# Softmax denominators of every second query chunk from ScalarE's accumulated exponentials

## The chip, the cores and the metric

The kernel runs on one core of a Trainium2 chip. Its engines work side by side, each through its own queue in program order: TensorE (PE in the profile; its weight loads are PEld), VectorE (DVE), ScalarE (ACT), GpSimd (POOL) and SyncE (SP), which issues most of the DMAs. The metric is the device time of one execution in microseconds; of several executions the median counts.

## The reference

It is a block of a transformer with the normalization after each part: attention without a mask, a residual and a layer norm, then a layer of eight low-rank experts of which each token uses one, a residual and a layer norm. With B = 4 sequences of S = 1024 tokens, width D = 512, 16 heads of 32, rank 64:

```
xq, xk, xv = heads(x @ wq.T), heads(x @ wk.T), heads(x @ wv.T)
probs = softmax(xq @ xk.T)                    # over the 1024 keys, no scaling
x = layernorm(x + merge(probs @ xv) @ wo.T)
logits = x @ Wr.T + br
e, weight = argmax(softmax(logits)), max(softmax(logits))
x = layernorm(x + weight * B[e] @ (A[e] @ x) / 64)
```

All of it is in 32-bit floats. The softmax takes 4 x 16 x 1024 rows of 1024 scores, and each row needs its maximum, its exponentials and their sum.

## The kernel before

**Units and steps.** A unit is a sequence b and a group g of four heads; there are 16. The queries of a unit come in four chunks of 256, the keys in eight tiles of 128. The program is a list of some 270 steps, and in step i every engine gets the work of two positions: `scores(i)`, and `weigh(i - 16)`, which works one unit behind. For the last sequence the order is turned: chunk by chunk, the four groups of a chunk after one another, so that finished chunks can go on to the experts.

**scores** (lines 280 to 297). For 128 queries and 512 keys TensorE makes the scores of four heads in four PSUM banks (L290), each from a strip of 32 rows, so that four matmuls run together. VectorE takes the maximum of each row from them (L292). After eight such steps, which are two chunks, the two halves' maxima are joined (L296), and GpSimd splits the result into three bf16 parts (`split`, L192 to L197), one column each of `spread_m`. Two steps later TensorE turns them (`turn_m`, L303) and ScalarE copies them as `mT`.

**weigh** (L313). For two key tiles and 256 queries TensorE first writes the negated maxima into four banks, as a product of ones and `mT` (L321), and adds the scores, keys down the partitions (L330). ScalarE takes the exponential of each bank (L340, 128x512), which are the weights `probs`. GpSimd adds the weights of key tile after key tile into `dens` (L343, L351), all but the last one, or for the last unit all but the last two.

**combine, settle, divide.** In every fourth step, when a chunk's eight key tiles are there, TensorE multiplies the weights with the values (L372, 32 matmuls for one bank), and ScalarE copies the result (L380). Two steps later `settle` sums over the partitions by matmuls with ones, of `dens` and of the tiles that GpSimd left out (L360), and ScalarE copies that too (L391). VectorE takes the reciprocal (L394, 128x256), and in the step after that GpSimd multiplies (L399) and has `aT`, the chunk's attention.

**PSUM.** There are eight banks, handed out in strict rotation by `bank()`. A matmul that opens a bank waits until whoever reads that bank's last content is done.

**What fills the steps.** Projections of queries, keys and values (L257, L267, L276, each followed by a ScalarE copy out of PSUM: L259, L268, L277), the product with `wo` (L455), and the experts: for the first three sequences tokens are sorted by expert through DRAM and each pair of tiles is turned (L601), taken up (L608), taken down (L617), normalized and stored (`step`, `weigh_y`, `norm_y`, `store`); the last sequence is computed for all experts at once and masked (`Last`: `project`, `norm`, `turn`, `up`, `mask`, `down`). The normalization itself is `apply` (L420) on ScalarE; its statistics are VectorE's (L415 to L417).

**What sets the order.** Each filling is a `Piece` with a cost in TensorE cycles, a first and a last step. A planner (lines 913 to 949) goes through the steps, works out a `level`, the mean cost that the steps must take for all pieces to meet their last step, and puts pieces into a step until it is reached. Steps with a combine are `busy` and get only pieces that are due. Within a step the order is `early` (loads), `ahead`, `weigh`, `scores`, `combine`, `small`, the pieces, `behind`. That order is then fixed for every engine:

```
if NS <= i < N:
    weigh(i - NS)
if i < len(maxima):
    scores(i)
if i in busy:
    u, c, _ = weights[i - NS]
    summed[u, c] = combine(u, c)
```

## Time and profile before

| | |
|---|---|
| median of 3 runs | 1534.2 us (1533.95 to 1535.69) |
| the profiled execution | 1532.2 us, its span 1530.5 us |
| granted TensorE clock, mean | 0.997 |
| GpSimd, running sums L351 and L343 | 745.3 + 150.9 us in 380 additions |
| VectorE, maxima L292 | 635.0 us in 1024 |
| ScalarE, exponentials L340 | 528.8 us in 1024 |
| TensorE, sums by ones L360 | 42.6 + 39.4 us busy |

In the profile a group is one line's instructions on one engine: output and inputs, shapes (partitions x elements), how many, their busy time together, the mean duration of one, and then the engine's idle time before them and who ended it. Instructions of one engine overlap at their edges, so the mean of one can be longer than busy time divided by their number. An fp32 matmul shows as two passes, and four of them in separate strips run together. A wait reads "who <- for whom: us in total, times, longest". The chain of work that ended last is followed back from the last instruction, at each step to what released it.

### The profile page before, as it was taken

Reading aid. Unit: us, or ns where it says so; the run is one execution under the profiler, and the core shown is the slowest. Engines: PE = TensorE matmul, PEld = TensorE weight load, DVE = VectorE, ACT = ScalarE, POOL = GpSimd, SP = SyncE. Lnnn points to the kernel's source line nnn. Section 1 sums busy time; section 2 is a strip of 40 time slices with the busy share of each in tenths; the row PEclk is TensorE's granted clock in tenths of the full one; section 3 lists DMA queues with packets and bytes.
Section 4 is the critical chain, followed back from the end, with each engine's and each line's share of the span. In section 5 each row is a group of like instructions: output and inputs, shape, how many; then the busy total and the mean of one; then the engine's idle time right before and its main releaser. Section 6 shows DMA issues by size and latency. Waiting matters only on the chain.

```text
span 1530.5 us, 37870 instructions
## 1 busy us (share of the span) xinstructions
PE 1495.6 (98%) x15571; PEld 965.1 (63%) x15571; DVE 929.0 (61%) x1733; ACT 763.2 (50%) x1583; POOL 1116.1 (73%) x939
## 2 busy tenths in 40 slices
PE   8999999999999999999999999999999999999996
PEld 6666666666666666666666666666666565665655
DVE  1556666656676457666677556766667567776323
ACT  1125555554445556555445555655445455555551
POOL 2028888877777777888777868888877777778880
PEclk9999999999999999999999999999999999999999
DMA  7431212132002423324100522441400331121000
GB/s 234 138 102 51 71 43 71 42 97 99 15 15 97 146 84 111 113 90 146 35 15 30 173 84 77 125 139 43 166 15 16 123 93 33 57 82 61 29 1 28
DMA packets 93054, 122.13 MB, mean 80 GB/s; under 512 B 7608, under 2 KB 68040, under 8 KB 92881
## 3 DMA queue, kind: packets, MB, share of 16 engines
q1 hardware_dynamic: 84672, 103.93, 21.6%
q0 software_dynamic: 6096, 13.69, 2.4%
q8 instruction: 122, 2.00, 0.6%
q10 hardware_dynamic: 2112, 2.10, 0.4%
q14 instruction: 52, 0.42, 0.1%
HBM read 92.34 MB, written 33.63 MB: 82 GB/s over the span
## 4 chain that ended last, share of the span: by engine, by line
PE 88%; POOL 4%; ACT 3%; issue 2%; DVE 2%; DMA 1%; ACTq 0%; POOLq 0%; SPq 0%; DVEq 0%
PE bank L372 14%; PE bank L290 14%; PE bank L330 13%; PE bank L276 8%; PE bank L257 8%; PE bank L267 8%; PE bank L455 7%; PE bank L321 5%; PE bank L360 4%; POOL dens L351 3%; ACT probs L340 2%; PE bank L601 2%; PE bank L617 2%; PE bank L608 2%; PE bank L729 1%
## 5 line engine op out<-in xcount | busy, mean ns | idle before, releaser
L292 DVE TENSOR_REDUCE top<-bank 128x1 f32<-128x512 f32 x1024 | 635.0, 682 | 458.9 <-PE bank L290 451.9
L351 POOL TENSOR_TENSOR dens<-dens,probs 128x1024 f32<-128x1024 f32 x316 | 745.3, 2358 | 128.7 <-ACT probs L340 116.4
L340 ACT ACTIVATE probs<-bank 128x512 f32<-128x512 f32 x1024 | 528.8, 603 | 286.2 <-PE bank L330 272.9
L290 PE MATMUL bank<-k,q 32*128 32x512 f32 x2048 | 287.1, 594 | 1.5 <-DVE whose_i L552 1.3
L330 PE MATMUL bank<-q,k 32*128 32x256 f32 x4096 | 266.9, 374 | 0.0
L372 PE MATMUL bank<-probs,v 128*32 128x256 f32 x4096 | 236.0, 381 | 0.8 <-ACT probs L340 0.8
L330 PEld LDWEIGHTS bank<-q,k 32*128 32x128 f32 x4096 | 201.4, 184 | 18.8 <-issue 3.2
L372 PEld LDWEIGHTS bank<-probs,v 128*32 128x32 f32 x4096 | 127.1, 110 | 125.9 <-ACT probs L340 47.9
L343 POOL TENSOR_TENSOR dens<-probs 128x1024 f32<-128x1024 f32 x64 | 150.9, 2358 | 62.7 <-ACT probs L340 62.4
L257 PE MATMUL bank<-xT,wq 128*128 128x256 f32 x512 | 129.2, 398 | 8.7 <-DMA xT<-in_xt 6.1
L290 PEld LDWEIGHTS bank<-k,q 32*128 32x128 f32 x2048 | 112.0, 184 | 25.8 <-issue 6.1
L267 PE MATMUL bank<-xT,wk 128*128 128x256 f32 x512 | 125.4, 389 | 1.4 <-ACT probs L340 0.9
L276 PE MATMUL bank<-wv,xT 128*128 128x256 f32 (+1 forms) x512 | 125.0, 391 | 0.6 <-ACT probs L340 0.2
L257 PEld LDWEIGHTS bank<-xT,wq 128*128 128x128 f32 x512 | 95.2, 194 | 47.4 <-ACT probs L340 25.7
L455 PE MATMUL bank<-wo,aT 128*128 128x264 f32 (+1 forms) x512 | 123.2, 389 | 1.7 <-POOL aT L399 1.7
L394 DVE RECIPROCAL both<-both 128x256 f32<-128x256 f32 x64 | 111.6, 1744 | 11.1 <-ACT both L391 11.1
L276 PEld LDWEIGHTS bank<-wv,xT 128*128 128x128 f32 x512 | 93.7, 190 | 36.6 <-ACT probs L340 18.9
L267 PEld LDWEIGHTS bank<-xT,wk 128*128 128x128 f32 x512 | 95.3, 192 | 33.8 <-ACT probs L340 21.1
L455 PEld LDWEIGHTS bank<-wo,aT 128*128 128x128 f32 x512 | 94.5, 190 | 32.8 <-ACT probs L340 16.8
L321 PE MATMUL bank<-mT,ones_b 3*128 3x512 bf16 x1024 | 107.5, 384 | 3.1 <-ACT probs L340 1.5
L380 ACT COPY both<-bank 128x256 f32<-128x256 f32 x64 | 23.9, 373 | 157.6 <-PE bank L372 151.6
L635 POOL DMA_INDIRECT out<-x x48 | 49.5, 1032 | 53.8 <-DMA out<-x 35.3
(124 smaller groups left out, 1038.4 us busy)
## 6 DMA issues: line engine op xcount, KB each, us to landing
xT<-in_xt SPq DMA_DIRECT2D x98, 512.0 KB, 3.6
sorted<-nothing SPq DMA_DIRECT2D x12, 1028.0 KB, 7.4
x<-sorted SPq DMA_DIRECT2D x48, 257.0 KB, 3.0
h<-in_x SPq DMA_DIRECT2D x32, 256.0 KB, 4.6
wa<-in_wa SPq DMA_DIRECT2D x48, 128.0 KB, 2.6
wb<-in_wb SPq DMA_DIRECT2D x48, 128.0 KB, 3.6
out<-h SPq DMA_DIRECT2D x8, 256.0 KB, 2.0
wo<-in_wo POOLq DMA_DIRECT2D x1, 1024.0 KB
```

The lines of the kernel that those rows point to most:

```text
L257: pe.matmul(ps, wq_sb[:, c, ts(units[u][1], P)], x.x[:, c, :], start=(c == 0), stop=(c == C - 1))
L267: pe.matmul(ps, wk_sb[:, c, ts(units[u][1], P)], x.x[:, c, :], start=(c == 0), stop=(c == C - 1))
L276: pe.matmul(ps, x.x[:, c, ts(t, P)], wv_sb[:, c, columns(h)], start=(c == 0), stop=(c == C - 1))
L290: pe.matmul(ps, q[r, ts(t % TQ, P)], kT[u][r, ts(n, 512)], start=True, stop=True)
L292: dve.tensor_reduce(top[i][:, here // 2, j, n : n + 1], ps, axis=AX.X, op=ALU.max, negate=True)
L321: pe.matmul(ps.rearrange("p (k q) -> p k q", q=QC), ones_b[r, :], m[r, :].unsqueeze(1).to_broadcast((NP, 2, QC)), start=True, stop=False,)
L330: pe.matmul(ps[:, ts(k, QC)], kT[u][r, ts(2 * kp + k, P)], qT[u, c][r, :], start=False, stop=(k == 1),)
L340: act.activation(pr[:, :, j, :], ps.rearrange("p (k q) -> p k q", q=QC), AF.Exp)
L343: pool.tensor_add(dens[u, c], pr[:, 0].rearrange("p j q -> p (j q)"), pr[:, 1].rearrange("p j q -> p (j q)"),)
L351: pool.tensor_add(dens[u, c], dens[u, c], pr[:, k].rearrange("p j q -> p (j q)"))
L372: pe.matmul(ps[j * HD : (j + 1) * HD, :QC], v[:, k, col : col + HD], probs[u, c, k // 2][:, k % 2, j, :], start=(k == 0), stop=(k == NK - 1),)
L455: pe.matmul(ps, aT[b, c, n][:, ts(i, P)], wo_sb[:, c, columns(half)], start=(c == 0), stop=(c == C - 1))
```

## The change

The chunks are taken in pairs, which share one `spread_m`. For the second chunk of each pair the sum of the weights is computed while its maxima are: ScalarE takes the exponential of the scores once more, from the banks of `scores`, with the maximum of that half row as its bias, and sums along the row (`accum_out`); the exponentials themselves go to a tile `junk` that nobody reads. When both halves are known, the sums are scaled to the common maximum and added, and VectorE takes the reciprocal (`invert`, one step later). The reciprocal goes the way of the maximum: it is split into three bf16 parts, in three more columns of `spread_m`, and turned by the same matmuls. For that chunk `combine` spreads it over the partitions by four bf16 matmuls with a constant `pick`, copies it, and VectorE multiplies it with the combined values. For the first chunk of a pair GpSimd now adds all eight key tiles, and `settle` (four matmuls, a reciprocal in PSUM, a multiply, all on VectorE after that) runs four steps after its combine, in the step in which the other chunk is combined.

The maxima of the two chunks take turns, step by step, so that the steps with exponentials of scores are the odd ones. Copies of q, k and v go from ScalarE to VectorE. `apply` goes to GpSimd, but for the last chunk of all. The planner's level is 1500 cycles higher in one of four steps (an odd one without a combine) and 750 lower in the others, queries may be projected a unit earlier, and the first and last steps and the gaps of the fillings behind a chunk become shorter. The core of the diff:

```diff
+    maxima = [(maxima[s - s % TS + s % 2 * KP + s % TS // 2], s % 2 * KP + s % TS // 2) for s in range(len(maxima))]
+    def summed_early(s):
+        return s % TS >= KP
...
-        act.copy(qT[u, x.n], ps)
+        dve.tensor_copy(qT[u, x.n], ps)
...
         for j, ps in enumerate(tiles):
-            dve.tensor_reduce(top[i][:, here // 2, j, n : n + 1], ps, axis=AX.X, op=ALU.max, negate=True)
+            dve.tensor_reduce(top[i][:, at, j, n : n + 1], ps, axis=AX.X, op=ALU.max, negate=True)
+        if at >= TQ:
+            for j, ps in enumerate(tiles):
+                act.activation(
+                    junk[:, j % 2, :],
+                    ps,
+                    AF.Exp,
+                    bias=top[i][:, at, j, n : n + 1],
+                    accum_out=sums[i][:, at - TQ, j, n : n + 1],
+                )
         if here == TS - 1:
+            m = spread_from[i % 2]
+            less = work.tile([P, TQ, GH, 2], F32, tag="less", name="less")
+            dve.tensor_reduce(m[:, :, :, 0], top[i], axis=AX.X, op=ALU.min)
+            dve.tensor_sub(less, m[:, TQ:, :, 0:1].to_broadcast((P, TQ, GH, 2)), top[i][:, TQ:])
+            act.activation(less, less, AF.Exp)
+            room[i] = m, less
+
+    def invert(i):
+        m, less = room[i]
+        dve.tensor_mul(less, less, sums[i])
+        dve.tensor_reduce(m[:, TQ:, :, 1], less, axis=AX.X, op=ALU.add)
+        dve.reciprocal(m[:, TQ:, :, 1], m[:, TQ:, :, 1])
+        split(m, [spread_m[i % 2][:, :, :, p : 2 * NP : NP] for p in range(NP)], "mrest")
...
+    def settle(s):
+        u, c, _ = weights[s]
+        b, g = units[u]
+        ps = bank()[:, :QC]
+        for j in range(GH):
+            pe.matmul(ps[j * HD : (j + 1) * HD, :], ones, dens[u, c][:, ts(j, QC)], start=True, stop=True)
+        dve.reciprocal(ps, ps)
+        aT[b, g, c] = work.tile([P, QC], F32, tag="aT", name="aT", bufs=15)
+        dve.tensor_mul(aT[b, g, c], ps, both[u, c])
+
+    def combine(s):
...
+        if summed_early(s):
+            ps = bank()[:, :QC]
+            for j in range(GH):
+                pe.matmul(
+                    ps[j * HD : (j + 1) * HD, :],
+                    pick[:, j, :],
+                    mT[s // TS][:, ts(s % TS // KP, QC)],
+                    start=True,
+                    stop=True,
+                )
+            inv = work.tile([P, QC], F32, tag="inv", name="inv", bufs=1)
+            dve.tensor_copy(inv, ps)
...
+        if summed_early(s):
+            aT[b, g, c] = work.tile([P, QC], F32, tag="aT", name="aT", bufs=15)
+            dve.tensor_mul(aT[b, g, c], ps, inv)
+        else:
+            both[u, c] = work.tile([P, QC], F32, tag="both", name="both", bufs=1)
+            act.copy(both[u, c], ps)
...
+    def apply(h, rs, i, eng=pool):
+        scale, shift = rs[:, 0, i : i + 1], rs[:, 1, i : i + 1]
+        if eng is act:
+            act.activation(h, h, AF.Identity, bias=shift, scale=scale)
+        else:
+            eng.tensor_scalar(h, h, scale, shift, ALU.mult, ALU.add)
...
     for i in range(len(weights) // TS):
+        later(TS * i + TS, 0, invert, i, where=ahead)
         later(TS * i + TS + 2, 512, turn_m, i)
...
+        level += 1500 if i % KP == 1 else -750
...
         if i in busy:
-            u, c, _ = weights[i - NS]
-            summed[u, c] = combine(u, c)
+            if summed_early(i - NS):
+                settle(i - NS - KP)
+            combine(i - NS)
```

## The prediction

> **What bounds the kernel now.** I read the busy times first, then the groups, the waits, the chain in a middle stretch, and the order of time in one step.
>
> ```profile
> span 1530.5 us, 37870 instructions
> PE 1495.6 (98%) x15571; PEld 965.1 (63%) x15571; DVE 929.0 (61%) x1733; ACT 763.2 (50%) x1583; POOL 1116.1 (73%) x939
> ```
>
> TensorE is busy for 98% of the span, at a granted clock of 0.997. Busy is not proof, so the waits decide:
>
> ```profile
> DVE top L292 <- PE bank L290: 451.9, 202, 24.2
> ACT probs L340 <- PE bank L330: 272.9, 226, 4.5
> ```
>
> In 202 of 256 steps VectorE stood waiting for the scores, and before 226 exponentials ScalarE stood waiting for TensorE. So TensorE sets the pace, and what it is spared is gained, until another engine makes it wait. The chain that ended last, in a middle stretch (start, us, what):
>
> ```profile
> 599.69 0.33 PE bank L321 x4
> 600.01 0.86 PE bank L330 x16
> 600.88 0.86 PE bank L290 x8
> 601.74 1.03 PE bank L360 x16
> 602.76 1.93 PE bank L257 x8
> ...
> 612.95 3.59 PE bank L372 x64
> ```
>
> A step is 0.33 + 0.86 + 0.86 = 2.05 us, then its fillings: 1.93 for a projection (1.75 for a second one), 3.59 for a combine in every fourth step, 1.03 for a settle. The same step in order of time elsewhere:
>
> ```profile
> 1100.69 0.40 PE L321 MATMUL bank<-mT,ones_b 3*128 3x512 bf16 x4
> 1100.92 1.03 PE L330 MATMUL bank<-q,k 32*128 32x256 f32 x16
> 1101.78 1.03 PE L290 MATMUL bank<-k,q 32*128 32x512 f32 x8
> 1102.06 2.07 ACT L340 ACTIVATE probs<-bank 128x512 f32<-128x512 f32 x4 [2.64 <-PE bank L330]
> 1102.85 2.47 DVE L292 TENSOR_REDUCE top<-bank 128x1 f32<-128x512 f32 x4
> ```
>
> Counted from the step's start: exponentials from 1.37 to 3.44 (0.52 each), maxima from 2.16 to 4.63 (0.62 each). A score bank is free today at 4.63 at the latest. The rows that price the change:
>
> ```profile
> L360 PE MATMUL bank<-probs,ones 128*32 128x256 f32 x544 | 42.6, 390 | 0.0
> L360 PE MATMUL bank<-dens,ones 128*32 128x256 f32 x512 | 39.4, 380 | 2.0 <-POOL dens L351 1.9
> L394 DVE RECIPROCAL both<-both 128x256 f32<-128x256 f32 x64 | 111.6, 1744 | 11.1 <-ACT both L391 11.1
> L420 ACT ACTIVATE x<-x,rs 128x512 f32<-128x512 f32 x48 | 36.8, 827 | 2.3 <-POOL rs L410 2.2
> 1497.95 1.52 ACT L420 ACTIVATE h<-h,rs 128x512 f32<-128x512 f32 x2 [11.51 <-POOL rs L410]
> ```
>
> **What TensorE is spared.** L360 has 544 + 512 = 1056 passes, 66 lots of 16 at 1.03: 68 us. Afterwards 32 settles of 8 passes stay, 0.52 each, and 32 picks of four bf16 matmuls of 256 columns come. The pick lies between 0.16 (half of L321's 0.33 for four of 512 columns) and 0.40 (L303, four of 128 columns that do not overlap: 0.40 in the order of time); I take 0.25. 32 x 0.77 = 25, so 43 us go (38 to 46). Both new items stand right ahead of the combine, in its tile shape. At the end the last division (copy, settle, reciprocal 1.75, multiply 0.72) made TensorE idle for 1.7 us; now one multiply of some 0.4 remains, under matmuls that need it last: 2 us. Spared: 45.
>
> **Waits that go.** In the stretch from 1442 to 1466 the chain is 69% GpSimd's L351: the running sums, 2.36 each, came too late for steps that hold little else. The four steps from 1446 to 1466 took 20 us, and their matmuls at the prices above 12. GpSimd's additions fall from 380 to 224, by 156 x 2.358 = 368 us, so I take 7 of the 8. At 1369 and 1377 the normalizations (L420, 0.76 each) stood ahead of exponentials on ScalarE; 84 of 88 go to GpSimd: 3 us. Together 10 (0 to 13).
>
> **What ScalarE gets.** 512 exponentials of scores, with a per-partition bias and a summed output, four in every odd step. Each waits for VectorE's maximum; queued behind it are the next step's exponentials and the copies of u, xsT and both, and TensorE waits for the banks of all of these. No row has this form. Below: 0.52, as L340. Above: 0.95, the 0.76 of L420, with two per-partition operands, and 0.19 for delivering the sum, as ScalarE's smallest activation (L436, 188 ns). I take 0.73: one such operand is half of the way from 0.52 to 0.76, and half of the 0.19. In total that is 374 us, against 174 us taken away (copies of q, k, v 72, of the sums 25.5, half of L380 12, L420 64): busy 763 becomes some 970, not a bound as a whole. In an odd step it is: 2.07 + 2.92 = 4.99, done 6.36 after the step's start.
>
> With eight banks in rotation the next step's scores need the last of these banks 1.19 us into that step, so an odd step shorter than about 5.2 makes TensorE wait. Most odd steps are long enough: two projections 5.7, combine 5.6 or 6.4. In the changed order 19 are not. Six have one projection (3.96): 1.03 each. Three hold an expert's up and its transposes (4.25) and seven also the down matmuls (5.3), with 1.36 of copies more on ScalarE: 2.1 and 1.05 each. Three others lack 5.2 together. Sum 25 us (9 at 0.52; at 0.95, 42 and more, see the rival).
>
> The Trainium skill, "ScalarE: Activation LUTs" (section "What ACT_TABLE_LOAD costs"), speaks against the move: a per-partition operand adds about 93 ns to an ACTIVATE. L340 to L420, with two of them, agrees roughly, 0.24 us a pair. By the page alone, with 0.61 and no price for the sum, the 25 would be an estimated 16 and the forecast 1511.
>
> **What VectorE gets.** 192 copies at about 0.40 (L457, PSUM to SBUF, 0.42 or 0.38 in a row), 77 us; 32 reciprocals fewer, minus 56; 96 short multiplies and copies, 38; 128 tiny ones at 0.2, 26. Busy 929 becomes some 1015. The copies stand behind the step's maxima and hide in the idle time that L292 shows. But all of the division falls into the 32 steps that settle two chunks: maxima until 4.63, minimum and difference 0.4, reciprocal 1.74, then three of some 0.42, the last at 8.1. The next step's scores want that bank at 6.4 + 1.2 = 7.6: 0.45 each, 14 us (0, if the eight banks happen to stand better, to 30). The expert steps hold 5.98 of VectorE's work against 5.3: 2 us for what spills over.
>
> GpSimd loses also 47 us of divisions (L399) and gains 84 normalizations, each between 0.6 (an 8x512 cast on GpSimd, 602 ns) and 1.2 (half of L351): 50 to 100 us. They stand ahead of its scatters and stores, at most a few us later; that, the five splits now after the reciprocal, and the loads that SP issues in another order (DMA share at most 0.39 from 90 us on) hide behind steps of slack: nothing, at worst 5 us.
>
> The skill's "TensorEngine Tiling (Array Packing)", section "PSUM Bottleneck", warns that packing speeds TensorE but not the emptying of PSUM. This case has both engines on score banks twice in odd steps. Applied to every odd step rather than to 19, with 0.45 us lost in each of 128, it would make an estimated 58 in place of the 25 and the time 1553.
>
> **Sum.** -45 - 10 + 25 + 14 + 2 = -14. The profiled execution took 1532.2 (span 1530.5 and 1.7 around it) and becomes 1518; the median of the runs is 2.0 above it, 1534.2, so I forecast 1520.
>
> **Rivals.**
> 1. ScalarE becomes the bound of odd steps: an exponential with its sum costs 0.95. Then the 19 steps lose 42; in the 32 combines without a settle ScalarE's copy frees its bank at 7.7 against 6.8, 0.88 each, 28 us; the 33 steps of two projections lose 0.45, 15; with 14 and 2 that is 101 against 55, so 1580. The balance tips at about 0.80, where the 19 steps and the copies cost 39. For it: L420 at 0.76 without any sum. Against it: L420 has two operands and writes what it reads.
> 2. ScalarE behind VectorE: the reciprocal of settle steps (VectorE 6.4 of 6.5 us) delays the next maxima, and every expert step does, so that exponentials wait. If each of 32 settles costs 1.0 instead of 0.45 and 12 expert steps 0.7, that is 24 us more: 1544. For it: at 1278 to 1288 the chain already runs through VectorE. Against it: VectorE waits for TensorE before 202 maxima.
> 3. The settles were no loss, or all of the gain returns as waits for banks: 1534. Against it: the chain passes through L360 in order, 1.03 us at a time.
> 4. Everything hides: 0.52 each, and no wait after the reciprocal: -55 + 9 + 2, so 1490.
>
> **How the numbers follow.** A difference of 0.2% is about what a measurement of this kernel can tell. The forecast's own case (1503 to 1530) has 0.46; rival 4 has 0.12; rival 3 has 0.08; rival 2 has 0.19; rival 1 0.15, some of it between its tipping point and its full price. Faster 0.58, same 0.08, slower 0.34. Most of 1 lies above 1558 and half of 4 below 1497: the range is 1497 to 1558.
>
> **What would show it.** The ones-times-sums matmuls fall to 256 passes. The new exponentials' row shows four in about 2.9 us; over 3.25 says rival 1, and TensorE's waits then name ScalarE. TensorE busy falls to some 1460 to 1480. VectorE's own idle before the maxima should stay above 300 us; if not, and if ScalarE waits mainly for VectorE, it is rival 2. In the last 90 us GpSimd should leave the chain. I would be wrong first in the 0.73 or in the 0.45.

## The result, and the profile after

The changed kernel takes 1540.85 us (median of six runs, 1538.29 to 1544.62), the kernel before 1534.25 in six runs beside it: a ratio of 1.0043 (95% interval 1.0027 to 1.0059). It is slower by 0.4%, where 1520 was forecast. Two later comparisons gave 1.0058 (1.0045 to 1.0071) and 1.0046 (1.0030 to 1.0063). The profiled execution took 1541.39 us at a granted clock of 0.989. One run of those below, the fourth of a_noscatter_2, took 2412.57 us at a granted clock of 0.556 and is left out.

The page of the changed kernel, its span and its busy times:

```profile
span 1539.4 us, 37695 instructions
PE 1493.6 (97%) x14899; PEld 972.3 (63%) x14899; DVE 1008.9 (66%) x2117; ACT 946.4 (61%) x2267; POOL 772.3 (50%) x809
```

VectorE's 1009 and ScalarE's 946 lie near the foretold 1015 and 970. TensorE's 1494 does not lie near its 1460 to 1480: it runs 672 instructions fewer (of the sums' 1056 passes 256 are left, as foretold) and is as busy as before. Matmuls that wait for a bank show as busy time here: the same 2048 passes of scores have 316.2 us (L319) where they had 287.1 (L290). So part of the gain has gone into such waits. The lower mean clock goes with the stalls: from 104.7 to 480 us it is 1.00 as before, and from 497 to 507 us, where engines stand still, 0.73; in a_noscatter_2, a run below without that stall, it is 1.00 there too. Its view of waits, the lines that carry the comparison (us in total, times, longest):

```profile
DVE top L321 <- PE bank L319: 303.4, 201, 6.3
...
DVE top L321 <- remote: 12.6, 1, 12.6
...
PE bank L370 <- ACT junk L324: 5.0, 17, 0.5
...
PE bank L739 <- POOL h L468: 3.3, 1, 3.3
PE bank L405 <- POOL dens L397: 3.2, 1, 3.2
```

VectorE still waits for TensorE before 201 maxima, as foretold. New are TensorE's 17 waits for the score exponentials. Its waits for GpSimd should have left and grew, to 3.3 and 3.2 us from 1.9 and 1.7. VectorE has one wait of 12.6 us, where it had one of 6.6, until "remote", a releaser that the profile can't name. The new exponentials, four in the order of time:

```profile
283.27 0.71 ACT L324 ACTIVATE junk<-bank,top 128x512 bf16<-128x512 f32 x1
283.84 0.23 ACT L324 ACTIVATION_READ_ACCUMULATOR junk<-bank,top 128x1 f32 x1
283.93 0.72 ACT L324 ACTIVATE junk<-bank,top 128x512 bf16<-128x512 f32 x1
284.50 0.24 ACT L324 ACTIVATION_READ_ACCUMULATOR junk<-bank,top 128x1 f32 x1
284.60 0.73 ACT L324 ACTIVATE junk<-bank,top 128x512 bf16<-128x512 f32 x1
```

One exponential and its sum are two instructions that overlap; the next pair starts 0.66 us later (283.27, 283.93, 284.60). I had priced it at 0.73.

To find where the time went I split the span into steps, each from its first L370 matmul (L321 in the kernel before) to that of the next step, and took from each step its matmuls at the prices of the prediction: 2.05 for the step, 1.93 for a projection and 1.75 for a second one, 3.59 for a combine, 1.02 for an expert's transposes or up, 1.05 for its down matmuls, 0.4 for the turned maxima. What is left is waiting, plus the settling, which is left in so that it can be compared. Sorted by kind of step, in us (number of steps), from the profiled executions:

| kind of step | before | changed |
|---|---|---|
| settling (with its matmuls) | 53.4 (49) | 21.7 (23) |
| the step after a settling | 4.9 (47) | 14.2 (24) |
| the step after a short odd step (under 5.2 us of matmuls) | -0.1 (1) | 24.0 (18) |
| around the scatters (steps 88-95, 150-159, 214-223) | 18.7 (28) | 29.7 (28) |
| steps from 240 on | 9.0 (31) | 6.9 (31) |
| combines without a settling, and others | 11.8 (99) | 12.1 (131) |

The first exponentials' step starts at 104.69 instead of 99.84: 1.5 of it is the first load of xT (TensorE's wait for it 7.6 against 6.1), the rest two projections (3.65 together) that the planner now does earlier and that are missing later. After the last step 48.0 us follow, against 51.6.

### The profile page after: what moved, and what is told of

It is laid out like the page before. It is cut to its first block, busy times and chain, and to the rows that moved or that the text cites. A ratio compares the mean times of both kernels' runs of the same rounds, so it can differ in the third digit from the quotient of the medians.

```text
span 1539.4 us, 37695 instructions
## 1 busy us (share of the span) xinstructions
PE 1493.6 (97%) x14899; PEld 972.3 (63%) x14899; DVE 1008.9 (66%) x2117; ACT 946.4 (61%) x2267; POOL 772.3 (50%) x809
## 4 chain that ended last, share of the span: by engine, by line
PE 85%; ACT 5%; issue 4%; DVE 2%; POOL 2%; DMA 1%; SPq 0%; ACTq 0%; POOLq 0%; DVEq 0%
PE bank L431 15%; PE bank L319 14%; PE bank L379 14%; PE bank L283 8%; PE bank L302 8%; PE bank L293 8%; PE bank L503 6%; PE bank L370 5%; ACT probs L389 4%; PE bank L762 2%; PE bank L777 1%; ACT junk L324 1%; PE bank L665 1%; PE bank L656 1%; POOL dens L397 1%
## 5 line engine op out<-in xcount | busy, mean ns | idle before, releaser
L321 DVE TENSOR_REDUCE top<-bank 128x1 f32<-128x512 f32 x1024 | 636.1, 683 | 318.3 <-PE bank L319 303.4
L389 ACT ACTIVATE probs<-bank 128x512 f32<-128x512 f32 x1024 | 529.2, 605 | 414.0 <-PE bank L379 405.9
L397 POOL TENSOR_TENSOR dens<-dens,probs 128x1024 f32<-128x1024 f32 x192 | 452.8, 2358 | 86.0 <-ACT probs L389 77.1
L324 ACT ACTIVATE junk<-bank,top 128x512 bf16<-128x512 f32 x512 | 347.8, 717 | 76.1 <-DVE top L321 75.9
L319 PE MATMUL bank<-k,q 32*128 32x512 f32 x2048 | 316.2, 600 | 2.5 <-DVE whose_i L600 1.2
L379 PE MATMUL bank<-q,k 32*128 32x256 f32 x4096 | 274.4, 378 | 1.1 <-issue 1.1
L431 PE MATMUL bank<-probs,v 128*32 128x256 f32 x4096 | 237.9, 384 | 4.7 <-ACT probs L389 3.9
L211 POOL CAST sm<-sf 128x32 bf16<-128x32 f32 x32 | 8.2, 256 | 423.5 <-DVE sf L345 404.0
L379 PEld LDWEIGHTS bank<-q,k 32*128 32x128 f32 x4096 | 204.8, 186 | 22.8 <-issue 7.5
L431 PEld LDWEIGHTS bank<-probs,v 128*32 128x32 f32 x4096 | 128.3, 111 | 114.3 <-ACT probs L389 32.3
L319 PEld LDWEIGHTS bank<-k,q 32*128 32x128 f32 x2048 | 129.3, 186 | 37.2 <-DVE aT L440 6.9
L370 PE MATMUL bank<-mT,ones_b 3*128 3x512 bf16 x1024 | 115.7, 386 | 6.1 <-ACT junk L324 5.0
L324 ACT ACTIVATION_READ_ACCUMULATOR junk<-bank,top 128x1 f32 x512 | 121.5, 237 | 0.0
L370 PEld LDWEIGHTS <-ones_b 3*128 3x128 bf16 x1024 | 28.6, 91 | 97.8 <-issue 97.2
```

The lines of the kernel that those rows point to most:

```text
L319: pe.matmul(ps, q[r, ts(t % TQ, P)], kT[u][r, ts(n, 512)], start=True, stop=True)
L321: dve.tensor_reduce(top[i][:, at, j, n : n + 1], ps, axis=AX.X, op=ALU.max, negate=True)
L324: act.activation(junk[:, j % 2, :], ps, AF.Exp, bias=top[i][:, at, j, n : n + 1], accum_out=sums[i][:, at - TQ, j, n : n + 1],)
L370: pe.matmul(ps.rearrange("p (k q) -> p k q", q=QC), ones_b[r, :], m[r, :].unsqueeze(1).to_broadcast((NP, 2, QC)), start=True, stop=False,)
L379: pe.matmul(ps[:, ts(k, QC)], kT[u][r, ts(2 * kp + k, P)], qT[u, c][r, :], start=False, stop=(k == 1),)
L389: act.activation(pr[:, :, j, :], ps.rearrange("p (k q) -> p k q", q=QC), AF.Exp)
```

## The experiments

Kernels of one group ran together on one chip; each is given as a ratio to the kernel before in the same group. In the group of a_level, a_noscatter, a_norm_dve and a_pace the kernel before took 1525.16, in the others 1531.4 to 1533.4.

### What ScalarE's part costs

```
-            sums[i] = work.tile([P, TQ, GH, 2], F32, tag="sums", name="sums")
+            sums[i] = all_one
...
-        if at >= TQ:
-            for j, ps in enumerate(tiles):
-                act.activation(
...
```

> The changed kernel without its 512 exponentials of scores (L324); their sums are replaced by a constant 1, so the denominators of every second chunk are wrong, and the time holds everything of the change but this work of ScalarE. Theory A (ScalarE's turn in the odd steps is the largest cost, through score banks that come free late, through the choice's exponential that queues behind it, and in the stretch from 487 to 507 us): the 19 short odd steps give back about 1.1 to 1.4 us each, 22 to 25, the three steps 78, 82 and 86 some 5, the stretch 487 to 507 up to 8. The time falls from 1541 to 1503 to 1513. Theory B (the loss lies with VectorE, GpSimd and the loads, and ScalarE's part is the foretold 25 or less): 1518 to 1530, and the stretch 487 to 507 us keeps its 20 us.

Measured: 1519.41 us, ratio 0.9911 (0.9881 to 0.9941), so 20 us below the changed kernel by ratios. That lies in theory B's range, and so does its place: the step after a short odd step falls from 24.0 us to 7.1, the settling and what follows it keep their times (22.8 and 13.9), and steps 91 to 93 still take 25.2 us against 26.4. Step by step the difference is what the prediction had priced. The six odd steps with one projection cost the next step 0.86 to 1.13 each (foretold 1.03); three with up and transposes 2.22, 2.13 and 1.69 (2.1); six of the seven with down as well 0.9 to 1.09 (1.05). The chain of the changed kernel (start, us, what) behind one of the first kind:

```profile
294.17 0.86 PE bank L379 x16
295.04 1.90 PE bank L319 x7
```

And the chain of a_nosum there:

```profile
292.83 0.86 PE bank L371 x16
293.69 0.86 PE bank L320 x8
```

The scores (L319, here L320) take 1.90 instead of 0.86, because their last banks are still held by ScalarE. One place had not been priced: in the steps 78, 82 and 86 VectorE stands inside the choice of experts for ScalarE's small exponential, which is queued behind the four large ones, 1.0 us each time.

### What a settling costs

```
-            [probs[u, c, k // 2][:, k % 2] for k in range(added(u), NK)]
-            + [dens[u, c].rearrange("p (j q) -> p j q", q=QC)],
+            [dens[u, c].rearrange("p (j q) -> p j q", q=QC)],
```

> The kernel before with TensorE summing only the running sum (16 passes, 1.03 us) in each chunk and leaving out the one or two key tiles that GpSimd had not added; the sums lack those tiles, everything else is as it was. It measures by itself what a pass spared on TensorE is worth. 544 of 1056 passes go: 34 lots at 1.03 are 35 us. Theory A (TensorE sets the pace): 1534 becomes 1498 to 1502. Theory B (the time comes back as waits for banks, sums or copies): 1515 to 1530.

Measured: 1518.02 us, ratio 0.9911 (0.9886 to 0.9935): 13.6 us, where theory A says 34 and theory B 4 to 19, so theory B. The prediction halves a settling of 16 passes, 1.03, to 0.52. The chain of this kernel:

```profile
594.93 0.05 issue
594.98 0.64 PE bank L360 x8
```

Eight passes take 0.64, with 0.05 ahead of them. So a settling gets 0.3 shorter and not 0.5, some 19 us in all of them by the profile, and 5 of these do not reach the end. The same in the changed kernel (settling L405, pick L417, then the combine), with the scores of the step behind it:

```profile
1098.00 0.57 PE bank L405 x8
1098.57 0.11 PE bank L417 x4
1098.68 0.18 issue
1098.86 3.66 PE bank L431 x64
1102.52 0.33 PE bank L370 x4
1102.84 0.86 PE bank L379 x16
1103.71 1.43 PE bank L319 x8
```

A step that settles has a median of 6.57 us, one that only combines 5.64: 0.93 where I had 0.77. The combine (L431) is 0.18 late and 0.07 longer than before. The 1.43 in the last line is the price of the divisions on VectorE, 0.57 over the usual 0.86: the last two weight loads of these scores wait until its last multiply (L440), which is queued behind the reciprocal.

```
+            if summed_early(i):
+                later(i + NS + 1, 4 * QC, settle, i - KP)
...
-            if summed_early(i - NS):
-                settle(i - NS - KP)
             combine(i - NS)
```

> The changed kernel with the settling of the even chunk one step later, so that its reciprocal (1.76 us on VectorE) no longer stands in the step of two divisions. Theory A (the 0.45 us foretold for each of 32 steps are really lost; the step after a settling took about 0.7 longer than its matmuls): 14 to 20 us faster than the changed kernel, 1521 to 1527. Theory B (VectorE's reciprocal only moves to the next step's maxima, or was hidden): within 4 us of 1541. The order of the pieces shifts a little with it (the short odd steps go from 26 to 23, up to 4 us), so less than 5 us of gain decides nothing.

Measured: 1580.04 us, ratio 1.0312 (1.0290 to 1.0334): 40 us slower than the changed kernel, outside both theories. The chain shows why:

```profile
624.29 0.91 PE bank L319 x8
625.19 0.61 DVE top L321
625.81 0.57 issue
626.38 1.28 DVE top L321 x2
627.66 1.68 DVE bank L406
629.34 0.02 issue
629.36 0.43 DVE aT L408
```

The reciprocal works in the settling's bank, and that bank is free only after four maxima, 1.68 and 0.43 on VectorE. One step later nothing long stands between: TensorE is through with its step and waits from 625.2 to 629.8. In the changed kernel the combine's 3.59 us cover this. The step after a settling lost 38.1 us in 24 steps instead of 14.2. The 0.45 of the prediction is thus the remainder of a good place, and not a loss that a later place would spare.

### GpSimd at the end

```
-    def apply(h, rs, i, eng=pool):
+    def apply(h, rs, i, eng=act):
```

> The changed kernel with all 88 normalizations on ScalarE, as before the change (827 ns each there against 772 on GpSimd). Theory A (GpSimd's queue, with the normalizations in front of the running sums and of the transposes' input, makes TensorE wait 3.3 at 1378 and 3.2 at 1463, with a lower clock behind each): the two waits go, 5 to 10 us faster, 1531 to 1536. Theory B (ScalarE is the fuller engine in these steps, so the normalizations delay its exponentials): 2 to 8 us slower, 1543 to 1549.

Measured: 1550.83 us, ratio 1.0120 (1.0099 to 1.0140), some 10 us slower than the changed kernel: theory B, and more. The step of the settling at 1463 does fall from 11.30 to 7.74, but four steps earlier a combine takes 10.00 instead of 4.78.

```
-                apply(self.h[i], self.rs, i, pool if self.n < NQ - 1 else act)
+                apply(self.h[i], self.rs, i, dve if self.n < NQ - 1 else act)
```

> The changed kernel with the normalizations of the last sequence (12 of 16 are on GpSimd) on VectorE. Theory A (at 1319 to 1328, 1378 and 1463 TensorE waits behind GpSimd's queue, in which these normalizations, 772 ns each and up to 1.5 together, stand with the experts' and with the running sums): the waits for h and for dens go, 6 to 10 us faster, 1531 to 1535. Theory B (the running sums themselves are what is late, or VectorE is as full as GpSimd in these steps): within 3 us of 1541.

Measured: 1535.09 us, ratio 1.0067 (1.0050 to 1.0084): by ratios no better than the changed kernel on other chips. The unaltered kernel did not run on that chip, so by the total nothing is decided, but its profile can be compared step by step: step 263 falls from 11.30 to 6.52 us, and step 260 grows from 3.12 to 12.25. VectorE in that step, in order of time:

```profile
1441.37 5.02 DVE L468 TENSOR_SCALAR h<-h,rs 128x512 f32<-128x512 f32 x2 [8.39 <-POOL rs L454]
```

It waits at the head of its queue for a statistic (L454) that GpSimd gets to only behind its sums. Whichever engine normalizes, the sums decide. The chain of the kernel before in the same stretch:

```profile
1451.18 2.35 POOL dens L351
1453.54 0.68 POOL aT L399
1454.22 2.33 POOL dens L351
1456.55 0.04 issue
1456.60 0.64 PE bank L360 x8
```

And that of the changed kernel:

```profile
1454.98 2.35 POOL dens L397
1457.33 1.52 POOL h L468 x2
1458.85 2.33 POOL dens L397
1461.18 0.07 issue
1461.24 2.35 POOL dens L397
1463.60 0.04 issue
1463.64 0.72 PE bank L405 x8
```

```
+            eng = dve if s >= len(weights) - NS else pool
...
-                    pool.tensor_add(dens[u, c], dens[u, c], w)
+                    eng.tensor_add(dens[u, c], dens[u, c], w)
```

> The changed kernel with the running sums of the last 16 steps (16 additions of 2.36 us on GpSimd) on VectorE, which has no maxima any more there. Theory A (halving GpSimd's additions over the whole kernel did not help at the end: an even chunk now needs all 8 tiles, 18.9 us, while its four steps hold some 16 us, and the settling at 1463 waits for them): steps 256 to 263 fall from 34.7 us to 28 to 30, 4 to 7 us faster than the changed kernel. Theory B (the wait at 1463 is for the normalization and the transposes' input, and VectorE only takes the additions' place in the queue): less than 2 us.

Measured: 1535.35 us, ratio 1.0010 (1.0002 to 1.0019), so 6.4 us less than the unaltered kernel beside it (1541.79): theory A. Steps 256 to 263 took 30.0 us instead of 34.8 (33.1 in the unaltered kernel beside it), and TensorE no longer waits for the sums. The profile has 14 of these additions and not 16: seven for a chunk of eight tiles, 16.5 us and not 18.9. Some 3 us of the difference of the two profiles lie elsewhere, in step 220 (8.4 for 11.5), where the edit changes nothing.

```
+        eng = dve if s >= len(weights) - NS else pool
...
-            pool.tensor_add(
+            eng.tensor_add(
...
-                    pool.tensor_add(dens[u, c], dens[u, c], pr[:, k].rearrange("p j q -> p (j q)"))
+                    eng.tensor_add(dens[u, c], dens[u, c], pr[:, k].rearrange("p j q -> p (j q)"))
```

> The kernel before with the running sums of its last 16 steps on VectorE, and nothing of the change. Theory A (the sums of 2.36 us each on GpSimd made TensorE wait between 1442 and 1466, as the chain of waits says): 5 to 9 us faster than the kernel before, and the chain leaves GpSimd there. Theory B (TensorE waits there for something else next): less than 2 us.

Measured: 1536.00 us, ratio 1.0015 (1.0006 to 1.0025): theory B. Steps 259 to 265 do take 28.8 us instead of 33.5, so GpSimd's sums cost the kernel before some 5 us there. But step 258 grows from 5.33 to 11.14: the sums, now on VectorE, delay its masking, and TensorE waits for that. So the run shows what the wait held, 5 us, but not that all of it would stay if the sums had gone from both engines. The line in its view of waits:

```profile
PE bank L730 <- DVE lu L725: 4.1, 2, 3.5
```

### The scatters

VectorE in the changed kernel's profile, two lines that follow each other in order of time:

```profile
490.50 2.48 DVE L321 TENSOR_REDUCE top<-bank 128x1 f32<-128x512 f32 x4
505.60 2.71 DVE L321 TENSOR_REDUCE top<-bank 128x1 f32<-128x512 f32 x4 [12.62 <-remote]
```

GpSimd in the same stretch:

```profile
485.65 9.64 POOL L397 TENSOR_TENSOR dens<-dens,probs 128x1024 f32<-128x1024 f32 x4 [1.29 <-ACT probs L389]
495.47 1.14 POOL L604 DMA_INDIRECT sorted<-h,slot_i  x1 [0.18 <-issue]
496.91 1.00 POOL L604 DMA_INDIRECT sorted<-h,slot_i  x1 [0.30 <-issue]
...
504.61 0.98 POOL L604 DMA_INDIRECT sorted<-h,slot_i  x1 [0.30 <-issue]
```

Eight scatters follow one another from 495.47 to 505.59, and VectorE starts its next maxima at 505.60, though their scores began at 498.0 and were done before 501. So of its 12.62 us some 7 are a stall; ahead of them it had no scores. In the kernel before the first four scatters of the third sequence ran from 1203.5 to 1208.5, with a wait of 6.62 until "remote" on VectorE.

> The changed kernel once more, unaltered, on the chip of the three runs beside it. In the profiled execution of the changed kernel VectorE stood for 12.6 us until 'remote' at 493 to 506, in that of the kernel before for 6.6 at 1203 to 1209; in four later executions of kernels with the same scatters, on another chip, there was no such wait. Theory A (that stall belongs to the change: eight scatters with nothing between them): the wait of 9 us or more is there again, and the ratio to the kernel before is 1.004 as in the first comparison. Theory B (it comes and goes with the execution and hits both kernels): the wait is absent or elsewhere, steps 91 to 93 take 16 to 18 us, and the ratio stays within 1.002 to 1.006 even so, since the kernel before is spared its own.

Measured, with nothing edited: 1541.79 us, ratio 1.0058; VectorE's wait is there again (11.95 us, until 504.93, before the train ends at 505.59). Theory A.

```
-            i = pool.indirect_dma_start(
-                out=sorted_x[self.b],
...
-                in_=self.h.pop(t),
...
-            self.scatters.append(i)
+            self.h.pop(t)
```

> The changed kernel without the 24 scatters of tokens (L604): the experts of the first three sequences read empty rows and their stores go nowhere, so the output of these sequences is missing; every other instruction is there. Theory A (a train of scatters on GpSimd with nothing between them is what holds VectorE for 12.6 us and ScalarE for 3.3 at 493 to 506, and something like it at 155 and 220): steps 91 to 93 fall from 26.4 us to 15 to 17, steps 155 to 157 and 219 to 221 lose 2 to 7 each; 14 to 20 us faster, 1521 to 1527, and the waits named 'remote' go. Theory B (the stall is VectorE's chain of the count, L575 to L600, and the copies behind it): steps 91 to 93 keep at least 22 us, and the time stays above 1535.

Measured: 1522.40 us, ratio 0.9980 (0.9971 to 0.9990). But on this chip the kernel before was 6 to 8 us faster than elsewhere, and none of the four profiles of this group has a wait until "remote", with scatters or without: in a_level and a_norm_dve, which have the same train of eight, steps 91 to 93 take 18.0 us. So this run doesn't tell the theories apart.

```
-                        then += [(5 + k // 4, 0, r.scatter, k) for k in range(NT)]
+                        then += [(5 + k // 4 if b else 10 + k // 2, 0, r.scatter, k) for k in range(NT)]
...
-                end + (20 + 4 * k if b < B - 2 else 19 + 3 * k),
-                after=[(p, 3 if k else 9)],
+                end + (20 + 4 * k if b == 1 else 23 + 3 * k if b == 0 else 19 + 3 * k),
+                after=[(p, 3 if k else 9 if b else 15)],
```

> The changed kernel with the first sequence's scatters five and more steps later, two in each of the steps 96 to 99, where GpSimd adds running sums between them; the experts of that sequence begin 5 steps later. Theory A (it is the train of eight scatters with nothing between that holds VectorE and ScalarE; the kernel before has its scatters in the same steps as running sums, in trains of four, and loses 2 to 7 us): steps 91 to 93 fall from 26.4 us to about 16, and steps 96 to 99 lose at most 3; 6 to 10 us faster, 1531 to 1535. Theory B (each scatter costs its time wherever it stands): steps 96 to 99 lose what 91 to 93 gain, within 3 us of 1541.

Measured: 1540.56 us, ratio 1.0093 (1.0075 to 1.0112), on the same chip. In this form the first expert's loads went out before the last two scatters, so some of its rows are not the sequence's own. For lack of the stall on that chip it says nothing on its cause; the later experts cost some time of their own. The open question was taken up again with four kernels on one chip:

> The changed kernel unaltered, beside the next three on one chip. Where VectorE's wait until 'remote' at 493 to 506 is there, the time is 1.004 to 1.006 of the kernel before; where it is absent, theory A (the wait is part of the loss) says 1.000 to 1.002, theory B (it is not) still 1.004 to 1.006.

Measured: 1540.02 us, ratio 1.0046. The wait is there, in other places: 6.7 us on ScalarE and 5.4 on VectorE, in step 93, which takes 12.18 us.

> The changed kernel without its 24 scatters, once more, on the chip of the unaltered one beside it (the first three sequences' experts read empty rows and their stores go nowhere, so the output lacks them). Theory A (the scatters make the waits until 'remote' and the losses at 91 to 93, 154 to 157 and 219 to 221): no such wait, 12 to 17 us faster than the unaltered kernel. Theory B (only the count's chain on VectorE is at fault): less than 4 us.

Measured: 1520.39 us (three runs), ratio 0.9928 (0.9907 to 0.9949): by ratios 18 us below the unaltered kernel beside it, and no wait until "remote". Theory A.

> The kernel before without its 24 scatters, with the same part of the output missing. Theory A (in the kernel before GpSimd's running sums stand between its scatters, and they cost it less): 4 to 8 us faster than the kernel before (its one long wait until 'remote' was 6.6). Then the scatters are worth 6 to 11 us of the difference between the two kernels. Theory B (they cost both the same): 12 us or more.

The same edit in the kernel before. Measured: 1524.51 us, ratio 0.9946 (0.9930 to 0.9963): 8 to 9 us, a little above theory A's. By ratios the scatters cost the changed kernel some 10 us more than the kernel before, give or take 5; the whole difference between the two kernels is 7 here. Without scatters the changed kernel is the faster one by some 3 us, which lies within the intervals. In the profiles 7 of the 10 us lie in the steps around the scatters, 5 of them in the first sequence, where the train of eight is.

The edit of a_pace with 16 in place of 15 steps, so that all scatters stand ahead of the loads:

> The changed kernel with the first sequence's scatters two in each of the steps 96 to 99, between GpSimd's running sums, and that sequence's experts 7 steps later (in the earlier form the first expert's loads went out before the last two scatters). Theory A (a train of eight with nothing between is what costs): where the unaltered kernel beside it waits until 'remote' at 493 to 506, here steps 91 to 93 take 16 to 18 us and 96 to 99 lose at most 3, so 6 to 10 us faster than it. Theory B (the scatters cost the same anywhere): within 3 us of it.

Measured: 1536.89 us, ratio 1.0024 (1.0012 to 1.0035), 3.1 us below the unaltered kernel: at theory B's edge by the total, and theory A's by the place. Steps 91 to 93 take 18.0 us (24.7 in the unaltered kernel beside it), steps 96 to 99 lose 1 us, and no wait until "remote" is left on VectorE. The second sequence's stretch lost 4 us more, where its experts now stand in other steps. GpSimd in this kernel, sums and scatters in turn:

```profile
521.39 1.14 POOL L604 DMA_INDIRECT sorted<-h,slot_i  x1 [0.18 <-issue]
522.83 1.00 POOL L604 DMA_INDIRECT sorted<-h,slot_i  x1 [0.30 <-issue]
523.83 4.82 POOL L397 TENSOR_TENSOR dens<-dens,probs 128x1024 f32<-128x1024 f32 x2
528.80 1.00 POOL L604 DMA_INDIRECT sorted<-h,slot_i  x1 [0.15 <-issue]
```

So scatters that go out two at a time between sums cost next to nothing (0.9 us), and eight in one train cost 6.7 us, on the chips that show the stall at all. Steps 91 to 93 take 24.7 us in a_again_2, against 18.0 here and without scatters (a_noscatter_2). The 26.4 of the first profile hold 1.7 more, from another cause: step 91 took 9.92 us there, at a granted clock of 0.83, and so it did in a_noscatter without a scatter (9.97). What holds VectorE and ScalarE during a train isn't shown by any run; in a_choose_behind VectorE stands idle for 10.2 us beside the train, and the profile names TensorE's projection as the releaser. Even without scatters step 91 takes 8.29 us against 6.34 in the kernel before: that is the count's chain on VectorE (L575 to L600), now ahead of a step with less in it.

### Versions

```
-        level += 1500 if i % KP == 1 else -750
+        level += 2200 if i % KP == 1 else -1100
```

> The changed kernel with the planner's odd steps filled further (+2200 and -1100 in place of +1500 and -750), nothing else. Of the 18 short odd steps (under 5.2 us of matmuls) between the first exponentials and the last stage 3 are left (69, 133, 197). Theory A (a short odd step makes the next step wait for ScalarE, 1.0 us behind one projection or an expert's up, down and transposes, 2.1 behind up and transposes): about 14 of them go, so 14 to 18 us, 1523 to 1528. Theory B (the time lost there comes back at the next narrow place: even steps become emptier, and VectorE or the score banks then wait there): 0 to 6 us, 1535 to 1541.

Measured: 1526.20 us, ratio 1.0001 (0.9992 to 1.0011). By ratios that is 6 to 9 us less than the changed kernel on other chips, at theory B's edge or beyond; but the unaltered kernel did not run on this chip, where the stall at the scatters is absent, so the ratio is a poor measure. With the steps around the scatters left aside the waits of the two profiles differ by some 9 us. The steps behind short odd ones lose 5.3 us instead of 24.0, so theory A holds for the place; of the 19 us some are lost again, most plainly at step 262, which takes 12.06 us because TensorE waits 8.9 for GpSimd's normalization.

```
-                later(i + abs(gap), cost, f, *args, where=ahead if gap < 0 else small)
+                where = behind if f.__name__ == "choose" else ahead if gap < 0 else small
+                later(i + abs(gap), cost, f, *args, where=where)
```

> The changed kernel with the choice of experts (L481 to L488) issued behind the projections of its step instead of ahead of them, for the first three sequences. Theory A (VectorE waits inside the choice for ScalarE's small exponential, which is queued behind the four score exponentials, and the projection's sum L505 stands behind that: 1.0 us in each of the steps 78, 82 and 86 and their like in each sequence): 3 to 9 us faster over the three sequences. Theory B (the wait only moves to the next step's maxima): within 2 us.

Measured: 1542.33 us, ratio 1.0049 (1.0032 to 1.0065): theory B. Steps 78, 82 and 86 each get 0.5 to 0.6 shorter and the steps ahead of them 0.4, and around the scatters 4 us are lost again.

> The changed kernel with four things together: odd steps filled further as in the run on the levels (there 6 us), the last running sums on VectorE, the choice behind the projections, and the experts' normalizations and stores one step later, as they stood before the change. If the losses add up as priced (6, 4 to 7, 3 to 9, and 0 to 4 of the 3.2 us that the transposes' input waited at 1378): 13 to 22 us faster than the changed kernel, a ratio of 0.990 to 0.996 to the kernel before. If they hide one another, no better than 1.000.

The edits of a_level, a_adds_dve and a_choose_behind, and

```
-                then=[(-1, 0, r.weigh_y, k - 2), (1, 0, r.norm_y, k - 2), (2, 0, r.store, k - 2)] if k >= 2 else [],
+                then=[(-1, 0, r.weigh_y, k - 2), (2, 0, r.norm_y, k - 2), (3, 0, r.store, k - 2)] if k >= 2 else [],
```

Measured: 1527.10 us, ratio 0.9961 (0.9947 to 0.9976), 14.7 us below the unaltered kernel beside it, at the lower end of the 13 to 22.

> The changed kernel with three things together, one for each cause found: odd steps filled further (6 us), the last running sums on VectorE (6), and the first sequence's scatters between GpSimd's running sums (3). If they add up: 15 us faster than the changed kernel, about 1526, a ratio of 0.994 to 0.996 to the kernel before. If they hide one another: 0.998 and more.

The edits of a_level, a_adds_dve and a_pace_2. Measured: 1525.80 us, ratio 0.9947 (0.9933 to 0.9961): faster than both kernels, by 0.5% than the one before. They add up in the total. Its profile (of the longest of its five runs, 1531.02) still has a wait until "remote", now in the second sequence (step 157, 15.06 us), whose scatters are not spread.

## Why the prediction was wrong

The sign was wrong, by 21 us. Against the terms of the sum:

| term | foretold | measured | from |
|---|---|---|---|
| settling and pick on TensorE | -43 | -37 | 66 lots at 1.01, less 32 at 0.93 |
| the tail | -2 | -3.6 | 48.0 for 51.6 |
| the start | 0 | +1 | 4.85 later, less 3.65 of matmuls moved there |
| waits that go | -10 | 0 to +3 | GpSimd's waits at 1378 and 1463; steps from 240 on |
| ScalarE | +25 | +20 | a_nosum |
| VectorE in the settling | +14 | +16 | 0.59 less 0.10, in 32 steps |
| GpSimd, loads, spill | +2, at worst 5 more | +10 | b_noscatter against a_noscatter_2 |
| sum | -14 | +6 to +9 | the medians: +6.6 |

The right-hand column adds terms from profiles and from ratios of runs, each good to some us; that the sum fits so well is partly luck.

**What held.** The two numbers that I named as most doubtful were good. The exponential with its sum comes every 0.66 us, where 0.73 was taken out of 0.52 to 0.95; the row of the profile that the prediction asked for (four in some 2.9 us) shows 2.65. So rival 1 falls. The places of the loss (odd steps under 5.2 us) and their prices, 1.03, 2.1 and 1.05, were met nearly one by one; only the "three others (5.2 together)" did not lose. That is partly luck. By the prediction's own terms the first price is 6.36 - 1.19 - 3.96 = 1.21 and not 1.03, and with 0.66 in place of 0.73 it is 0.93: two errors nearly cancel. The page "ScalarE: Activation LUTs" of the Trainium skill (section "What ACT_TABLE_LOAD costs") gives 93 ns for the operand. The trace is near it: L324 took 717 ns and L389 605, so 0.11 us, though L324 also writes bf16 and sums. By that figure alone an exponential would come every 0.61 us, an estimate; the rows show 0.66, with the separate read of the sum (237 ns) in it. The warning of "TensorEngine Tiling (Array Packing)" (section "PSUM Bottleneck") would have made an estimated 58 of the 25, and a_nosum measured 20. a_settle_later shows a loss of that kind: TensorE waited while VectorE kept a bank for 2.1 us.

**What failed first: "the waits that go, -10".** The step reads "GpSimd's additions fall from 380 to 224, by 156 x 2.358 = 368 us, so I take 7 of the 8". That is an average over chunks of two kinds. The odd chunks lost all of their additions and the even ones gained one, seven for six: a chunk that GpSimd sums now needs all eight tiles, since TensorE no longer takes the last, so its additions come one after the other at 2.36 us as they did before. Where the steps are short, from 1449 to 1463, the chain runs through L397 just as it had run through L351. a_adds_dve shows that it is these sums. Less their settlings (8 of 1.03 before, 3 of 0.93 now) the steps from 240 on lost some 3 us more than before, where 10 less was foretold. The 8 was also misread: from 1446 to 1466 the kernel before does the matmuls of five steps and not of four, 17 us and not 12 at the prediction's prices, so that 3 us were to be had there; b_adds_dve found 4.7 in the steps 259 to 265. And in that run VectorE's masking was late next. The prediction named the wait and did not ask what stood behind it.

**Second: "nothing, at worst 5" for what is moved on GpSimd and SP.** I had the scatters a few us late and hidden by steps of slack. In the kernel before running sums lay between them in most places. In the first sequence of the changed kernel they fall into a chunk that has no sums, so GpSimd issues all eight in one train, and VectorE and ScalarE stand beside it. By a_noscatter_2 and b_noscatter all scatters together cost some 10 us more than before, 5 of them in this place. The DMA share, which I put at 0.39 at most, was 0.50 from 840 to 880 us in the kernel before; whether the loads cost anything no run shows. It was to be seen in the changed order of GpSimd's instructions that the sums between the scatters were gone; what a train costs was to be guessed at best from the one wait of 6.62 in the profile of before.

**Third: "32 settles of 8 passes stay, 0.52 each", the pick 0.25.** The eight passes took 0.57 (0.64 in b_fewer_sums, against 1.00 for 16) and the pick only 0.11, together less than the 0.77. What the term left out is behind them: the combine waits 0.18 for the last exponential and takes 0.07 longer. 0.93 instead of 0.77 in 32 steps is 5 us.

**Of the rivals** 2 and 3 came nearest by the time (1544 and 1534) and neither is the cause: VectorE's loss was the foretold one, and the banks' too. (The 24 us of rival 2 are 26 by its own terms, 32 x 0.55 + 12 x 0.7.) What did not come was gains, 16 us of them, and a loss of 10 at the scatters had no term.

## What to carry to other kernels

When work is halved on an engine, ask in which order the remaining half comes: where it was dense, it may stay as dense as it was, and an average saving does not reach that place. Look also at what the removed instructions had been keeping apart, for a queue without them may send a train of transfers. And before a wait is counted as gain, name the engine that is late next; one run that takes away that wait in the kernel before, as b_adds_dve does, would have shown that 5 us lay there and that VectorE was next.

## What was not expected of the hardware

- Beside a train of eight scatters (1.0 us of GpSimd each, 1.3 apart) VectorE stood idle for 11.2 to 12.6 us in three executions, some 5 of them for want of scores. In the changed kernel's profile it started again with the train's end (505.60 and 505.59), in other executions between 3.0 us before it and 1.7 behind it. On one chip two kernels with the same train (a_level, a_norm_dve) lost nothing there, and the kernel before was 6 to 8 us faster, about what it gains elsewhere when its scatters are left out (8 to 9).
- The same short stop of TensorE (1.2 us in step 91, behind the count's chain on VectorE) was followed by a granted clock of 1.00 in some executions (step 91: 8.28 us, a_again_2, a_level) and by 0.83 in others (9.9 us, a_again, a_noscatter).
- Halving the passes of a short group of matmuls (16 to 8, 128x32 by 128x256) took its time in the chain from 1.00 to 0.64.
- On VectorE a normalization of 128x512 took 546 ns in the median of 12, but four that ran beside GpSimd's sums took 1.7 to 2.6 us. Each of these four ended 0.28 us after one of the sums had: at 1338.34, 1340.82, 1443.91 and 1446.39 us, behind sums that ended at 1338.06, 1340.54, 1443.63 and 1446.11. So VectorE's instruction waited for GpSimd's there; through what, no run shows.
- An exponential with a summed output shows as two rows, 717 and 237 ns, of which 0.66 us of ScalarE's time are left after overlap.
